# Layer 0 of a four-layer graph network: the general way is chosen before the heads instead of after them

## The chip, the cores and the metric

The kernel runs on one core of a Trainium2 chip. The metric is the device time of one execution in microseconds (us). A core has five engines that run their own instruction queues side by side[...]: TensorE (PE, matrix products; PEld is its weight load), VectorE (DVE), ScalarE (ACT), GpSimd (POOL) and SyncE (SP, which here only starts DMA transfers). Sixteen DMA engines move data between the chip's memory and the core's own buffers. A letter q behind an engine (SPq, ACTq, DVEq) names its sequencer: DMA starts, semaphores, register loads and branches.

## The reference

There are 4096 nodes with 256 features and one 0/1 adjacency matrix of 4096 x 4096, about 0.8% of it ones. Four layers follow each other; each adds its result to its input and normalizes. The change is in layer 0, a graph attention with 8 heads of 32 features:

```
node_feats   = (x @ W.T + b).reshape(4096, 8, 32)
logit_parent = (node_feats * a[None, :, :32]).sum(-1)
logit_child  = (node_feats * a[None, :, 32:]).sum(-1)
attn_logits  = leaky_relu(logit_parent[:, None, :] + logit_child[None, :, :], 0.2)
attn_logits  = where(adj[..., None] != 0, attn_logits, 0.0)
attn_probs   = softmax(attn_logits, axis=1)
out          = einsum('ijh,jhc->ihc', attn_probs, node_feats)
x            = layernorm(x + out)
```

A node that is not a neighbour keeps the logit 0 and so still has weight in the softmax. Layer 1 that follows is `x = layernorm(x + (diagonal(adj) + adj) @ (x @ weight) + bias)`; layers 2 and 3 are not touched by the change.

## The kernel before, in words

Nodes are cut into NB = 32 blocks of P = 128 rows. Layer 0 has two ways to the same result.

**The quick way** uses that exp(leaky_relu(p + c)) is exp(p) exp(c) where p + c is at least 0 and exp(0.2 p) exp(0.2 c) elsewhere, so that the softmax sums become matrix products with masks of zeros and ones. `sums0` (lines 383 to 530) makes the node features, the row factors `fac` (in `factors0`), the number `fits`, the column factors of all heads, written by the ACT queue to the DRAM tensor `gmd`, and then the dense products of the whole adjacency with the small-slope factors: for each pair of row blocks 16 loads of the adjacency, a cast on DVE, a byte copy of the adjacency on ACT stored to `nad` by the POOL queue, and 256 matrix products (line 517). Its result per row block, `zd`, is stored by the ACT queue (line 530). `src`, 132 KB in each partition, is read by these products to the end.

`layer0` (lines 214 to 333) then runs the heads: a loop over the two halves of four heads, in it over four stretches `it` of 1024 rows, in it over the four heads of the half. `na`, the adjacency bytes of a stretch (4 MB in 8 loads), and `gm`, the column factors of the half (6.5 MB in 8 loads, each with all four heads of 4 blocks), are loaded by SP in turns (lines 261 to 264). For a head and a group of 4 column blocks, ACT (groups 0, 1, 3, 4, 6) or DVE (groups 2, 5, 7) compares the row logits with the column logit and writes the mask `sg` (lines 292 and 285), DVE joins it bit by bit with `na` to `gt` (lines 294 and 287), and PE does 32 products of `gt` with `gm` into the accumulator `acc` (line 300),[...] it has two buffers. DVE reduces it, multiplies with `fac`, adds `z` (loaded from `zd` by the POOL queue, line 274) and divides (lines 305 to 316). In the second half the row block is added to `X` and normalized, by POOL during later heads, and for the last stretch by DVE at once (line 331).

**The general way**, `general0` (lines 532 to 690), computes the softmax with its true maxima for every head and row. It is needed only where the exponents would not fit; `fits` says so. It is called in `choose0` (line 335), inside a branch at run time (line 337), which stands between layer 0 and layer 1. There it replaces `X` by its own result. Each engine loads `fits` into a register and takes the branch for itself; where the body is left out, it raises its semaphore by what the body would have added, and SP besides waits for eight DMA counters.

`layer1` (lines 698 to 740) turns each four blocks of `X` (line 108), copies them (line 109), multiplies them by the weight (line 710), splits the product into a rounded and a rest part in `XD` (lines 126 and 127), and then multiplies the adjacency, loaded from `nad` by the ACT queue (line 188) and scaled by DVE and ACT (lines 205 and 203), with `XD` (line 731). The pieces are stored back as `adjs` by SP (lines 160 to 167).

**What sets the order.** The framework's planner orders the instructions of each engine's queue by priority (mostly the order of the program) and by its own estimate of when their inputs are ready; it may move an instruction ahead of older ones that wait. It does not move anything across a run-time branch. Buffers are placed on a stack: a buffer that lies where an older one lay waits for the older one's last user.

Of the kernel before, what the change touches and what calls it, by code (L numbers as in the profile page):

```python
# [9 lines left out]
F32 = mybir.dt.float32  # L10
I32 = mybir.dt.int32
F32R = mybir.dt.float32r
BF16 = mybir.dt.bfloat16
# [10 lines left out]
P = 128  # L24
# [31 lines left out]
class Net:  # L56
# [157 lines left out]
    def layer0(self):  # L214
        nc, tc, NB, D, N = self.nc, self.tc, self.NB, self.D, self.N
        H, C = 8, 32
        C1 = C + 1
        IT = min(1024, N)
        Q = IT // P
        keep = self.ctx.enter_context(tc.tile_pool(name="l0k", bufs=1, space=DRAM))  # L220
        self.fits = keep.tile([1, 1], I32, name="fits")
        with ExitStack() as ctx:
            pool = ctx.enter_context(tc.tile_pool(name="l0", bufs=1))
# [6 lines left out]
            fac = pool.tile([P, 4, NB, H], F32, name="fac")  # L230
            lpd = dram.tile([H, N], F32, name="lpd")

            def row_logits(t, h, it):
                nc.gpsimd.dma_start(t, bass.AP(tensor=lpd.tensor, offset=lpd.offset + h * N + it * IT, ap=[[0, P], [1, IT]]))
                return t
# [5 lines left out]
            zd = dram.tile([NB, P, H, C1], F32, name="zd")  # L241
            yd = dram.tile([NB, P, D // 2], F32, name="yd")
            gmd = dram.tile([2, P, NB, H // 2, 6 * C1], BF16, name="gmd")
            self.sums0(both, nlc, fac, lpd, nad, zd, gmd, lambda: row_logits(first, 0, 0))

            self.open_x()
            self.load1()
            X, xr = self.X, self.rows(self.x)
            gp = ctx.enter_context(tc.tile_pool(name="l0gm", bufs=1))
            work = ctx.enter_context(tc.tile_pool(name="l0w", bufs=2))  # L250
            psum = ctx.enter_context(tc.tile_pool(name="l0ps", bufs=2, space=PSUM))
            K = 4
            gm = gp.tile([P, NB, H // 2, 6 * C1], BF16, name="gm")
# [4 lines left out]
            for half in range(2):  # L258
                for it in range(N // IT):
                    i0 = it * Q  # L260
                    for g in range(NB // K):
                        nc.sync.dma_start(na[:, g * K:(g + 1) * K], nad[it, :, g * K:(g + 1) * K, :])
                        if it == 0:
                            nc.sync.dma_start(gm[:, g * K:(g + 1) * K], gmd[half, :, g * K:(g + 1) * K])
                    if half:
                        nc.sync.dma_start(X[:, i0:i0 + Q, :], xr[:, i0:i0 + Q, :])
                        y0 = work.tile([P, Q, D // 2], F32, name="y0", bufs=1)
# [1 line left out]
                    y = work.tile([P, Q, H // 2, C], F32, name="y")  # L269
                    for hh in range(H // 2):  # L270
                        h = half * (H // 2) + hh
# [48 lines left out]
                    y = y.rearrange("p q h c -> p q (h c)")  # L320
# [5 lines left out]
                    for q in range(0, Q, 2):  # L326
                        xs = X[:, i0 + q:i0 + q + 2, :]
# [4 lines left out]
                        else:  # L332
                            later.append(xs)

    def choose0(self):

        with self.tc.If(self.nc.values_load(self.fits, min_val=0, max_val=1) == 0):
            self.general0()

    def factors0(self, wp, ps, both, nlc, fac):  # L340

# [187 lines left out]
                    nc.vector.tensor_add(zt[:, 0], zt[:, 0], zt[:, 1])  # L529
                    nc.scalar.dma_start(zd[b + q], zt[:, 0])  # L530

    def general0(self):

        nc, tc, NB, D, X = self.nc, self.tc, self.NB, self.D, self.X
        H, C = 8, 32
        C1 = C + 1
        IT = 512
        Q = IT // P
        G = min(8, NB)
        with ExitStack() as ctx:  # L540
            pool = ctx.enter_context(tc.tile_pool(name="l0", bufs=1))
            work = ctx.enter_context(tc.tile_pool(name="l0w", bufs=2))
            nfa = pool.tile([P, NB, H, C1], F32, name="nfa")
            lp = pool.tile([P, NB, H], F32, name="lp")
            lc = pool.tile([P, NB, H], F32, name="lc")
            lc02 = pool.tile([P, NB, H], F32, name="lc02")

            xr = self.rows(self.x)
            for g in range(NB // 4):
                nc.sync.dma_start(X[:, 4 * g:4 * g + 4, :], xr[:, 4 * g:4 * g + 4, :])  # L550

            with ExitStack() as pre:
                wp = pre.enter_context(tc.tile_pool(name="l0pre", bufs=1))
                ps = pre.enter_context(tc.tile_pool(name="l0ps", bufs=2, space=PSUM))
                w0 = self.load_w(wp, self.w0t, "w0")
                b0 = self.load_row(wp, self.b0, "b0")
                a_bc = wp.tile([P, 2, H, C], F32, name="a_bc")
                for s in range(2):
                    nc.scalar.dma_start(
                        a_bc[:, s],  # L560
                        bass.AP(tensor=self.a0.tensor, offset=self.a0.offset + s * C,
                                ap=[[0, P], [2 * C, H], [1, C]]))
                nc.vector.memset(nfa[:, :, :, C:C1].rearrange("p b h c -> p b (h c)"), 1.0)
                for g in range(NB // 4):
                    xT = self.transposed(ps, wp, X[:, 4 * g:4 * g + 4, :], "xT")
                    for q in range(4):
                        b = 4 * g + q
                        pn = ps.tile([P, 512], F32, name="ps_nf")
                        for c in range(2):
                            nc.tensor.matmul(pn[:, :D], xT[:, c, q * P:(q + 1) * P], w0[:, c, :],  # L570
                                             start=(c == 0), stop=(c == 1))
                        nf = nfa[:, b, :, 0:C]
                        nc.vector.tensor_add(nf, pn[:, :D].rearrange("p (h c) -> p h c", h=H),
                                             b0.rearrange("p (h c) -> p h c", h=H))
                        for s, dst in ((0, lp), (1, lc)):
                            prod = wp.tile([P, H, C], F32, name="prod", bufs=2)
                            nc.vector.tensor_mul(prod, nf, a_bc[:, s])
                            nc.vector.tensor_reduce(dst[:, b, :], prod, AX.X, ALU.add)
                nc.vector.tensor_scalar_mul(lc02.rearrange("p b h -> p (b h)"),
                                            lc.rearrange("p b h -> p (b h)"), 0.2)  # L580
# [8 lines left out]
            with tc.For_i(0, NB, Q) as i0:  # L589
# [20 lines left out]
                hz = work.tile([P, Q], F32, name="hz")  # L610
                nc.vector.tensor_scalar(hz, zs[:, :, 0, C], 0.0, -BIG, op0=ALU.is_equal, op1=ALU.mult)

                y = work.tile([P, Q, D], F32, name="y", bufs=1)

                def largest(h):

# [31 lines left out]
                def attend(h, bc, e0):  # L648

                    po = ps_o.tile([C1, IT], F32, name="po")  # L650
                    for g in range(NB // 2):
                        e1 = ep.tile([P, 2, IT], F32, name="e1", bufs=3)
                        e2 = ep.tile([P, 2, IT], F32, name="e2", bufs=2)
                        for k in range(2):
                            jc = 2 * g + k
                            nc.scalar.activation(e2[:, k, :], bc[:, 1, :], AF.Identity, bias=lc02[:, jc, h:h + 1])
                            nc.vector.scalar_tensor_tensor(e1[:, k, :], bc[:, 0, :], lc[:, jc, h:h + 1], e2[:, k, :],
                                                           op0=ALU.add, op1=ALU.max)
                        jc = 2 * g
                        pen = pens[jc // G][:, jc % G:jc % G + 2, :]  # L660

                        nc.vector.tensor_tensor(e1, e1, pen, ALU.min)
                        nc.scalar.activation(e1, e1, AF.Exp)
                        for k in range(2):
                            jc = 2 * g + k
                            nc.tensor.matmul(po, nfa[:, jc, h, :], e1[:, k, :],
                                             start=(jc == 0), stop=(jc == NB - 1))
                    oT = work.tile([C1, IT], F32, name="oT")
                    nc.scalar.copy(oT, po)
                    pt = ps_t.tile([P, 512], F32, name="pt")  # L670
                    for q in range(Q):
                        nc.tensor.transpose(pt[:, q * C1:(q + 1) * C1], oT[:, q * P:(q + 1) * P],
                                            self.ident[:C1, :C1])
                    o = work.tile([P, Q, C1], F32, name="o")
                    nc.vector.tensor_mul(o, zs[:, :, h, :], e0.unsqueeze(2).to_broadcast([P, Q, C1]))
                    nc.vector.tensor_add(o, o, pt[:, :Q * C1].rearrange("p (q c) -> p q c", q=Q))
                    r = work.tile([P, Q], F32, name="r")
                    nc.vector.reciprocal(r, o[:, :, C])
                    nc.vector.tensor_mul(y[:, :, h * C:(h + 1) * C], o[:, :, :C],
                                         r.unsqueeze(2).to_broadcast([P, Q, C]))  # L680

                ahead = largest(0)
                for h in range(H):
                    now, ahead = ahead, (largest(h + 1) if h + 1 < H else None)
                    attend(h, *now)

                xs = X[:, bass.ds(i0, Q), :]
                nc.vector.tensor_add(y, y, xs)
                self.layernorm(work, y, y)
                nc.vector.tensor_copy(xs, y)  # L690


    def load1(self):
# [1154 lines left out]
@with_exitstack  # L1848
def tile_adj_resnorm(ctx: ExitStack, tc: tile.TileContext, args, out: bass.AP):
    net = Net(ctx, tc, args, out)  # L1850
    net.constants()
    net.adj_space()
    net.out_space()
    net.layer0()
    net.choose0()
    net.open_split()
    net.layer1()
    net.layer2()
    net.layer3()
# [41 lines left out]
```

## Time and profile before

| | |
|---|---|
| median of 3 runs | 4065.89 us (4064.93 to 4076.77) |
| the profiled execution | 4074.96 us, its span 4072.8 us |
| busy in the span | PE 96%, PEld 83%, DVE 74%, ACT 68%, POOL 26% |
| dense sums | to 598.0 us (last product of line 517) |
| heads | 613.8 to 1331.2 us (first and last product of line 300) |
| layer 1 | from 1350.1 us (first transpose of line 108) |
| bytes moved | 555.89 MB, mean 136 GB/s |

The profile is one execution. Its times are counted from the start of the span, which lies 2.2 us under the execution's own time; the execution itself lies 9 us above the median of the three runs. A row of the waits reads "who waited, on which line, for whom: us in total, how often, the longest". "issue" stands for time in which the profile shows no awaited engine. A row of the stretches gives from and to, the length, and for each engine its busy time and instructions, then the clock granted to TensorE, the mean busy share of the DMA engines and their GB/s.

### The profile page before, as it was taken

What the parts mean: (1) busy time and instruction counts of PE and PEld (TensorE: products, weight loads), DVE (VectorE), ACT (ScalarE), POOL (GpSimd) and SP (SyncE); (2) the same over time, 40 slices, a digit from 0 to 9 for tenths busy, and PEclk for the clock granted to TensorE, in tenths of its full rate; (3) what the DMA queues carried; (4) which work ended last, traced back from release to release, by engine and by line L of the source; (5) the groups of instructions that cost most, each with busy time, mean ns of one, the idle gap of its engine ahead of it and who ended that gap; (6) DMA issues with size and microseconds to landing.
All of it is one profiled execution on the core that took longest, in us unless ns stands there. A gap on an engine that the chain in (4) does not pass through costs nothing. (4 is left out here: it accounts for less than half of the span.)

```text
span 4072.8 us, 68706 instructions
## 1 busy us (share of the span) xinstructions
PE 3910.6 (96%) x25081; PEld 3381.8 (83%) x25081; DVE 2994.7 (74%) x6647; ACT 2755.4 (68%) x5127; POOL 1073.3 (26%) x1318
## 2 busy tenths in 40 slices
PE   7999989999999799799999999988999999999899
PEld 6999989999999688458888888864888888888677
DVE  7642328999999344548787877847899999999364
ACT  5543329999998222348888888834888888888132
POOL 0111110110333022301111111113455555555211
PEclk9999999999999899899999999999999999999999
DMA  4765555324221497333333333363333333335541
GB/s 122 226 212 177 179 176 189 96 80 148 73 86 48 186 374 306 117 110 92 100 96 95 101 95 103 106 221 96 108 105 117 103 108 115 103 111 190 181 160 47
DMA packets 291193, 555.89 MB, mean 136 GB/s; under 512 B 38966, under 2 KB 115382, under 8 KB 286742
## 3 DMA queue, kind: packets, MB, share of 16 engines
q1 hardware_dynamic: 208672, 394.61, 30.2%
q0 software_dynamic: 27664, 84.44, 6.2%
q10 hardware_dynamic: 54502, 72.27, 5.2%
q8 instruction: 203, 3.33, 0.3%
q14 instruction: 152, 1.25, 0.1%
HBM read 385.25 MB, written 165.94 MB: 135 GB/s over the span
## 5 line engine op out<-in xcount | busy, mean ns | idle before, releaser
L1301 PE MATMUL ps_a<-X,aT 128*128 128x256 f32 x4096 | 972.5, 380 | 1.3 <-ACT h L1442 1.1
L1301 PEld LDWEIGHTS ps_a<-X,aT 128*128 128x128 f32 x4096 | 775.6, 190 | 128.0 <-issue 3.5
L300 PE MATMUL acc<-gm,gt 128*128 128x198 bf16 x8192 | 704.1, 248 | 29.0 <-issue 15.8
L300 PEld LDWEIGHTS <-gt 128*128 128x128 fp8e4 x8192 | 700.4, 97 | 32.6 <-issue 16.0
L292 ACT ACTIVATE sg<-lpb,nlc 128x1024 fp8e4<-128x1024 f32 x640 | 671.3, 1135 | 60.9 <-DVE gt L294 35.0
L179 PE MATMUL ps_r<-XD,adj_piece 128*128 128x512 f32 x1952 | 548.9, 416 | 5.2 <-DMA adj_piece<-adjs 5.2
L517 PE MATMUL pz<-src,ar 128*128 128x264 f32 x4096 | 510.1, 287 | 10.4 <-DVE ar L507 8.2
L517 PEld LDWEIGHTS pz<-src,ar 128*128 128x128 f32 x4096 | 507.2, 190 | 13.2 <-DVE ar L507 12.5
L1028 ACT ACTIVATE ja<-e,nc 128x2048 uint8<-128x2048 f32 x240 | 481.0, 2004 | 2.0
L1294 ACT COPY aT<-ps_tp 128x512 f32<-128x512 f32 x512 | 295.8, 578 | 229.6 <-PE ps_tp L1292 227.5
L179 PEld LDWEIGHTS ps_r<-XD,adj_piece 128*128 128x128 f32 x1952 | 346.3, 190 | 79.3 <-issue 13.4
L510 ACT ACTIVATE nb<-a 128x512 uint8<-128x512 f32 x256 | 156.9, 630 | 292.7 <-DMA a<-in_adjt_dram 288.7
L1093 DVE MAX8 cand<-v 128x8 f32<-128x256 f32 x1024 | 347.2, 412 | 4.4
L1143 DVE SCALAR_TENSOR_TENSOR e<-e,edge 128x512 f32<-128x512 f32 x512 | 347.2, 750 | 2.2
L1292 PE MATMUL ps_tp<-ident,e 128*128 128x128 f32 x2048 | 308.4, 273 | 0.1
L1089 DVE SCALAR_TENSOR_TENSOR v<-e,hi 128x2048 f32<-128x2048 f32 x128 | 300.3, 2346 | 2.4
L1292 PEld LDWEIGHTS ps_tp<-ident,e 128*128 128x128 f32 x2048 | 257.2, 142 | 51.9 <-issue 0.9
L935 PE MATMUL ps_logit<-kT,q 128*128 128x512 f32 x1024 | 277.0, 412 | 15.0 <-DVE kT L893 7.6
L285 DVE TENSOR_SCALAR sg<-lpb,nlc 128x1024 fp8e4<-128x1024 f32 x384 | 283.2, 774 | 2.0
L937 ACT ACTIVATE e<-ps_logit 128x1024 f32<-128x1024 f32 x256 | 259.8, 1025 | 30.5 <-PE ps_logit L935 28.8
L507 DVE CAST ar<-a 128x1024 fp32r<-128x1024 f32 x128 | 88.6, 692 | 230.1 <-PE pz L517 230.0
L731 PE MATMUL ps_adj<-XD,adj_piece 128*128 128x512 f32 x1024 | 236.1, 391 | 0.0
(382 smaller groups left out, 5492.0 us busy)
## 6 DMA issues: line engine op xcount, KB each, us to landing
adj_piece<-adjs SPq DMA_DIRECT2D x552, 256.0 KB
a<-in_adjt_dram SPq DMA_DIRECT2D x256, 256.0 KB
adjs<-adj_piece SPq DMA_DIRECT2D x96, 512.0 KB
na<-nad SPq DMA_DIRECT2D x64, 512.0 KB
nad<-nb POOLq DMA_DIRECT2D x128, 128.0 KB, 3.3
lpb<-lpd POOLq DMA_DIRECT2D x32, 512.0 KB, 4.2
na<-nad ACTq DMA_DIRECT2D x16, 1024.0 KB
gmd<-gb ACTq DMA_DIRECT2D x64, 198.0 KB
```

The costliest lines, as they stand in the source:

```text
L179: nc.tensor.matmul(ps, a[:, k, :], rhs(jc).rearrange("p s d -> p (s d)"), start=(jc == 0), stop=(jc == self.NB - 1))
L285: nc.vector.tensor_scalar(sg[:, k, :], lpb, nlc[:, jc, h:h + 1], 2.0 ** -5, op0=ALU.is_ge, op1=ALU.mult, saturate=False)
L292: nc.scalar.activation(sg[:, k, :], lpb, AF.Sign, scale=-1.0, bias=nlc[:, jc, h:h + 1], saturate=False)
L300: nc.tensor.matmul(acc[:, q, :6 * C1], gt[:, k, q * P:(q + 1) * P], gm[:, jc, hh, :], start=(jc == 0 and q % 2 == 0), stop=(jc == NB - 1 a ...
L517: nc.tensor.matmul(pz[q][:, t, :W], ar[:, q, k, :], src[:, jc, t, s], start=(jc == 0 and s == 0), stop=(jc == NB - 1 and s == 1))
L1028: nc.scalar.activation(ja, e[:, s * HALF:(s + 1) * HALF], f, bias=nc1, accum_out=fs[:, i + s:i + s + 1])
L1089: nc.vector.scalar_tensor_tensor(v, ec, hi, ec, op0=ALU.is_lt, op1=ALU.mult, accum_out=sb[:, s:s + 1])
L1093: nc.vector.max(cand[:, 8 * j:8 * j + 8], v[:, k * 256:(k + 1) * 256])
L1143: nc.vector.scalar_tensor_tensor(ec, ec, edge[:, j:j + 1], ec, op0=ALU.is_ge, op1=ALU.mult)
L1292: nc.tensor.transpose(pt[:, k * P:(k + 1) * P], e[:, jc * P:(jc + 1) * P], self.ident)
L1294: nc.scalar.copy(aT, pt)
L1301: nc.tensor.matmul(pa[:, :D], aT[:, k * P:(k + 1) * P], X[:, jc, :], start=(jc == 0), stop=(jc == NB - 1))
```

## The change

The branch moves from the end of layer 0 to between `sums0` and the heads. The general way no longer writes `X`: it loads its own copies of `x`, writes its attention result, with a one in the 33rd place of each head, to `zd`, clears `gmd` and the two rows of `fac` that scale the head products, and leaves the addition and the norm to the heads. With the products scaled by nothing, the heads divide `z` by one. On the data of this task `fits` is 1 and the body is left out, before and after.

The second part is the order of the loads of `gm`: in each half the factors of its first head are loaded first, in turns with `na`, a group of 4 blocks at a time (for each partition four runs of 396 bytes in place of one of 6336), and then those of the other three heads, 8 blocks at a time.

```diff
             self.sums0(both, nlc, fac, lpd, nad, zd, gmd, lambda: row_logits(first, 0, 0))
+            self.choose0(fac, zd, gmd)
 
             self.open_x()
             self.load1()
...
                     for g in range(NB // K):
                         nc.sync.dma_start(na[:, g * K:(g + 1) * K], nad[it, :, g * K:(g + 1) * K, :])
                         if it == 0:
-                            nc.sync.dma_start(gm[:, g * K:(g + 1) * K], gmd[half, :, g * K:(g + 1) * K])
+                            nc.sync.dma_start(gm[:, g * K:(g + 1) * K, 0], gmd[half, :, g * K:(g + 1) * K, 0])
+                    for hh in range(1, H // 2 if it == 0 else 0):
+                        for g in range(0, NB // K, 2):
+                            nc.sync.dma_start(gm[:, g * K:(g + 2) * K, hh], gmd[half, :, g * K:(g + 2) * K, hh])
...
-    def choose0(self):
+    def choose0(self, fac, zd, gmd):
 
         with self.tc.If(self.nc.values_load(self.fits, min_val=0, max_val=1) == 0):
-            self.general0()
+            self.general0(fac, zd, gmd)
...
-    def general0(self):
+    def general0(self, fac, zd, gmd):
...
-            for g in range(NB // 4):
-                nc.sync.dma_start(X[:, 4 * g:4 * g + 4, :], xr[:, 4 * g:4 * g + 4, :])
-
...
                 for g in range(NB // 4):
-                    xT = self.transposed(ps, wp, X[:, 4 * g:4 * g + 4, :], "xT")
+                    xs = wp.tile([P, 4, D], F32, name="xs", bufs=2)
+                    nc.sync.dma_start(xs, xr[:, 4 * g:4 * g + 4, :])
+                    xT = self.transposed(ps, wp, xs, "xT")
...
-                y = work.tile([P, Q, D], F32, name="y", bufs=1)
+                y = work.tile([P, Q, H, C1], F32, name="y", bufs=1)
+                nc.vector.memset(y[:, :, :, C:], 1.0)
...
-                xs = X[:, bass.ds(i0, Q), :]
-                nc.vector.tensor_add(y, y, xs)
-                self.layernorm(work, y, y)
-                nc.vector.tensor_copy(xs, y)
+                nc.sync.dma_start(zd[bass.ds(i0, Q)].rearrange("b p h c -> p b h c"), y)
+
+            none = pool.tile([P, 4, gmd.shape[-2] * gmd.shape[-1]], BF16, name="none")
+            nc.vector.memset(none, 0.0)
+            for half in range(2):
+                for g in range(NB // 4):
+                    nc.sync.dma_start(gmd[half, :, 4 * g:4 * g + 4].rearrange("p b h c -> p b (h c)"), none)
+            nc.vector.memset(fac[:, 0:2], 0.0)
...
     net.layer0()
-    net.choose0()
     net.open_split()
     net.layer1()
```

More of the change, by code (lines that the diff above doesn't have):

```diff
@@ L530, in sums0 @@
                     nc.scalar.dma_start(zd[b + q], zt[:, 0])
-    def general0(self):
-        nc, tc, NB, D, X = self.nc, self.tc, self.NB, self.D, self.X
+    def general0(self, fac, zd, gmd):
+        nc, tc, NB, D = self.nc, self.tc, self.NB, self.D
         H, C = 8, 32
@@ L540, in general0 @@
         with ExitStack() as ctx:
-            pool = ctx.enter_context(tc.tile_pool(name="l0", bufs=1))
-            work = ctx.enter_context(tc.tile_pool(name="l0w", bufs=2))
+            pool = ctx.enter_context(tc.tile_pool(name="l0n", bufs=1))
+            work = ctx.enter_context(tc.tile_pool(name="l0nw", bufs=2))
             nfa = pool.tile([P, NB, H, C1], F32, name="nfa")
@@ L678, in attend @@
                     nc.vector.reciprocal(r, o[:, :, C])
-                    nc.vector.tensor_mul(y[:, :, h * C:(h + 1) * C], o[:, :, :C],
+                    nc.vector.tensor_mul(y[:, :, h, :C], o[:, :, :C],
                                          r.unsqueeze(2).to_broadcast([P, Q, C]))
```

## The prediction

> **What bounds the kernel now.** The page first: TensorE (PE) is busy for 96% of the span, so time is won only where PE stands still. Its chain of waits holds no waiting worth a per cent. I therefore went by stretches around the two seams of layer 0, then to the waits in each, then to the lines of the branch.
>
> The first seam (dense sums to heads). Columns of the stretches: PE, PE's weight load, VectorE (DVE), ScalarE (ACT) and GpSimd (POOL) busy, granted clock, DMA share, GB/s.
>
> ```profile
> 595.00:600.00 5.00, 2.99 (x25) 2.78 (x23) 3.66 (x11) 1.10 (x1) 0.65 (x1) 1.00 0.18 37
> 600.00:605.00 5.00, 0.00 (x0) 0.00 (x0) 0.74 (x1) 2.23 (x3) 2.29 (x4) 0.55 0.95 349
> 605.00:610.00 5.00, 0.00 (x0) 0.00 (x0) 0.00 (x0) 0.00 (x0) 0.00 (x0) 0.50 1.04 360
> 610.00:615.00 5.00, 1.23 (x8) 1.16 (x9) 2.55 (x4) 3.73 (x4) 0.00 (x0) 0.50 1.01 379
> ...
> 630.00:640.00 10.00, 9.89 (x115) 9.72 (x116) 5.10 (x6) 9.91 (x10) 0.00 (x0) 1.00 1.06 370
> ```
>
> PE has nothing to do from 598.0 to 613.8 while the DMA engines are full, and stay full until 643. The waits between 598 and 665 say what stood in line:
>
> ```profile
> PE acc L300 <- issue: 15.8, 1, 15.8
> ...
> ACT sg L292 <- issue: 9.0, 2, 8.8
> ...
> DVE gt L287 <- DMA na<-nad: 1.2, 1, 1.2
> ```
> and SP's own queue between 560 and 720:
> ```profile
> SPq L262 <- DMA zd<-zt: 7.4, 1, 7.4
> SPq L262 <- DMA w<-in_w_dram: 7.3, 1, 7.3
> ```
>
> ACT makes three masks at 598.9 to 602.5 and stops: its next instruction is the load of w1 (line 115), which starts at 610.29, in the same instant as SP's load that waited for a zd store issued at 599.95. That store needed 10 us behind 3.9 MB of na and gm. The fourth mask, hence the first gt, comes at 612.4 to 613.7. Head 0 ends with the reduction at 642.34; its 256 matmuls at 83.2 ns need 21.3 us. The seam costs 642.3 - 598.0 - 21.3 = 23 us of PE.
>
> The second seam (heads to layer 1), waits between 1325 and 1400, and then the lines of the branch (min/median/max ns, first and last start):
>
> ```profile
> PE ps_tp L108 <- DVEq L337: 19.0, 1, 19.0
> ...
> L337 ACTq COMPARE_BRANCH  x1: 50/50/50, 1315.5 to 1315.5; - x1
> L337 ACTq EVENT_SEMAPHORE  x1: 17/17/17, 1319.5 to 1319.5; - x1
> ...
> L337 PEldq COMPARE_BRANCH  x1: 3447/3447/3447, 1330.2 to 1330.2; - x1
> ...
> L337 DVEq TENSOR_LOAD <-fits x1: 722/722/722, 1346.0 to 1346.0; - x1
> ...
> L337 DVEq COMPARE_BRANCH  x1: 72/72/72, 1346.8 to 1346.8; - x1
> L337 DVEq EVENT_SEMAPHORE  x1: 21/21/21, 1349.8 to 1349.8; - x1
> ```
>
> PE's last head matmul ends at 1331.15, its next instruction starts at 1350.08. Between them DVE runs the last head's closing arithmetic and the norm of the last eight row blocks (to 1346.76), then needs 3.0 us for the branch. PE, ACT and POOL had passed; all wait for DVE, because the branch's body may write X. No engine stops the others at the branch; each loads fits itself, jumps, and counts itself through.
>
> [...] 2.9 us on DVE, 3.9 on ACT, 3.4 on PE. [...] the hardware queues' single packets take 13 ns at 128 B, 18 at 256, 27 at 512, 46 at 1024, 67 at 1584, 159 at 4096 and 241 at 6336 (medians of the packet records), a straight line. [...] the trace shows 0.50 in both pauses.
>
> **The change, part by part.**
>
> *First seam, wait added.* Everything behind the branch that uses memory of the general way, or reads zd and gmd, waits until the engines are through it. PE: 1331.15 to 1333.8 before, so 598.0 + 2.7 = 600.7. DVE: last zt 599.92 + 3.0 = 602.9. ACT: its last instruction is the zd store issued at 599.95 (ends 600.28), then load 0.65, branch[...]: 605.0. SP: it must see all outstanding hardware DMAs land (it waits on eight counters there), the zd store among them[...]. POOL is idle from 588. Last is ACT: na's first load starts at 605.0 instead of 598.87, 6.1 us later. Queued behind: all na and gm loads on SP, z and lpb loads on POOL, the w1 and bias loads and the masks on ACT.
>
> *First seam, wait removed.* The zd stores have landed before any load starts, so the 7.4 us hold of SP and the 7.8 us hold of ACT go. ACT: w1 and bias issues (0.41 + 0.49) then masks without a pause, 4.28 us per group of four (1.07 each). Groups 0, 1, 3, 4, 6 are ACT's: ready at 606 + 4.28 x 1..5 = 627.4, plus 1.23 for gt. PE takes groups in order at 2.66 us; group 6 from 628.6, group 7 ends at 634.
>
> *First seam, loads.* Head 0 needs na (4 MB: 1024 packets x 159 ns / 16 engines = 10.2 us) and its own quarter of gm in runs of 396 B. Between 256 and 512 B the records give 23 ns: 4096 x 23 / 16 = 5.9 us. With lpb and z (about 3 us) that is 19 us: all there at 605 + 19 + 2 = 626, before group 7 needs it at 631. Before it was 10.2 + 15.4 us and later. Bounds of a run: 18 ns, and 46 (as dear as 1 KB; 11.8 us, data at 632, still no loss over 1). The other heads' gm is 12 DMAs per half behind it, 17.7 us, needed from 634 on; hidden under head 0 and 1. SP issues 12 more DMAs in each half (28 for 16); at 0.32 to 0.55 us each (the 256-run loads of line 957 take 0.55) that is under 7 us of a queue which then idles until 681. ACT and DVE no longer have a lead over PE when PE starts, and both are over 96% busy in the first half, so I take 2 us off for hiccups. Head 0 ends at 634 to 636 against 642.3: gain 6. Bounds: 0 (first load at 611) and 9.
>
> *Half change.* Before: PE 100% busy from 900 to 1000. The new loads of the first head need 16 us instead of 26 and are released group by group over a head of 21 us. Cost 0; uncovered it would be a few us, once.
>
> *Second seam.* No branch, and X is not written by the general way: groups 0 to 5 of layer 1 (row blocks 0 to 23, last normed by POOL at 1298) can be turned and multiplied while DVE finishes. Their buffers: the accumulator's banks of head 30 are free since 1313; XD lies over fac and gm, read last at 1333.7. So PE idles 2 to 3 us rather than 19. Layer 1's eight groups took 1350.1 to 1373.6, 2.9 us each; six fill 17.6 us, the last two wait for the norm, which gets slower by the 24 split subtractions of 0.42 us on DVE (10 us, into a stretch of 15.6 where DVE is busy 11.7). End of the groups: 2.6 + 8 x 2.9 = 26 us after PE's last head matmul, against 42.5: 16; I take 2 off, because the layer's first pieces wait for na loads (DMA share 0.9 to 1.0 from 1350 to 1390, DVE waited 10.4 us for na) which gain less than PE. Gain 14. Bounds: 3.0 (only the branch goes) and 20 (PE never cold).
>
> *The general way itself* (its loads of x, its store to zd, cleared gmd and fac) doesn't run: fits is 1, as the trace shows no instruction of it.
>
> *Sum.* 6 + 14 = 20. The profiled execution took 4074.96 us (span 4072.8, 2.2 around it): 4055. It lies 9 above the median of the runs, 4065.89, so the forecast there is 4046.
>
> **The rivals.**
>
> (a) *The second seam stays shut*: layer 1 still waits for the whole norm, by the order the planner writes or by memory. For it: one queue per engine, ACT's na loads may stand before its copies. Against: after the branch, products and support are already mixed line by line. Only the branch is saved: 6 + 3 = 9, 4057.
>
> (b) *The first seam doesn't pay*: the loads start 6 us later and head 0 ends 6 later than now, at 648. For it: DMA share 1.0 up to 643. Against: the bytes wanted first fall from 10.5 to 5.6 MB. 14 - 6 = 8, 4058.
>
> (c) *More*: PE stays warm at the second seam and ACT passes the branch as fast as DVE: 9 + 20 = 29, 4037.
>
> (d) *Slower*: small runs become the bound. Place: head 0 of each half. At y ns per run its data come at 605 + 13 + 0.256y + 2 and are wanted at 631; at the half change the slack is some 25 us. The loss 0.512y - 36 eats the 20 at y = 109 ns and makes it 12 us slower at y = 133, some six times the 23 that the records give. For it: no packet of this size on these queues. Against: the straight line from 128 to 6336 B. With y = 135: 4079.
>
> **How the numbers follow.** Forecast 0.68 (4038 to 4053), (c) 0.08, (a) 0.12, (b) 0.05, (d) 0.07. About 0.3% or 12 us is what a measurement of this kernel can tell from no change; the three runs of before themselves spread by 12. Faster: 0.68 + 0.08 = 0.76; same: (a) + (b) = 0.17; slower: (d) 0.07. The range 4033 to 4060 leaves out (d), a third of (c), and the worse part of (a) and (b): under 0.15.
>
> **What would show it.** The branch's lines near 584 to 605; first na load at 605, first gt at 610 to 612, no 7 us waits for zd or w; head 0's reduction at 634 to 637; lines 108 and 710 start within 3 us of the last head matmul while DVE still norms; no PE wait for a branch there. Wrong if ACT is held again after the branch, if gm packets take far over 23 ns, if the transposes of layer 1 stand behind the last norm, or if the planner puts layer 1's copies among the last heads' masks and PE falls under 95% there.

## The result: 0.28% faster, little more than half of what was forecast

| | before | after |
|---|---|---|
| median of 17 runs each, side by side | 4070.23 us (4062.77 to 4076.77) | 4056.93 us (4049.9 to 4069.3) |
| ratio, 95% interval | | 0.9972 (0.9965 to 0.9979), 11.4 us less |
| the profiled execution | 4074.96 us | 4049.9 us |

The forecast was 20 us less. The time measured, 4057, is in the stated range, and it is the time that rival (a) gives, "6 + 3 = 9, 4057". To the microsecond that is luck: the rival counts from the 4065.89 us of three runs, and beside 17 runs the kernel before took 4070.23. In differences the forecast was 20, rival (a) 9, and 11.4 was measured.

The two profiled executions lie 24.6 us apart in their spans, twice the real difference. So the profiles were cut at marks that both kernels have, and the stages compared one by one:

| stage (us) | before | after | difference | forecast |
|---|---|---|---|---|
| last dense product to head 0's reduction | 44.34 | 39.67 | -4.7 | -6 |
| head 0's reduction to the last head product | 688.77 | 687.95 | -0.8 | 0 |
| last head product to layer 1's last adjacency product | 302.35 | 294.12 | -8.2 | -14 |
| the rest (layers 2 and 3) | 2439.4 | 2430.1 | -9.3 | 0 |

The first three rows make 13.7 us, inside the interval of the ratio (8.5 to 14.2 us). The fourth is not the change's: nothing is changed there, and before, after and the seven kernels below, whose layers 2 and 3 are the same, spread from 2426.5 to 2439.4 in it. The dense sums also happened to end 1.7 us sooner (596.3 against 598.0).

**The profile after.** From the page: the busy line, and the group of the head products.

```profile
PE 3903.3 (96%) x25081; PEld 3379.7 (83%) x25081; DVE 2995.7 (74%) x6647; ACT 2757.0 (68%) x5127; POOL 1072.1 (26%) x1318
...
L304 PE MATMUL acc<-gm,gt 128*128 128x198 bf16 x8192 | 704.3, 249 | 23.3 <-DVE gt L298 15.9
```

The shares are those of before: a change of 0.3% can't be read from them. (Lines have moved: the products of the heads are line 304 now, na's load is 263, gm's are 265 and 268, the branch is 341, layer 1's first products are 718 and its adjacency products 739.)

The first seam of after, in stretches with the columns of the prediction:

```profile
595.00:600.00 5.00, 1.32 (x11) 1.10 (x9) 2.98 (x9) 0.00 (x0) 0.00 (x0) 0.99 0.19 61
600.00:605.00 5.00, 0.00 (x0) 0.00 (x0) 0.75 (x1) 1.27 (x2) 2.72 (x4) 0.50 0.35 99
605.00:610.00 5.00, 0.69 (x5) 0.63 (x6) 1.97 (x3) 5.00 (x6) 0.48 (x1) 0.50 1.02 268
610.00:615.00 5.00, 4.24 (x29) 3.78 (x28) 2.47 (x3) 5.00 (x6) 0.00 (x0) 0.64 1.05 347
615.00:620.00 5.00, 4.12 (x49) 4.11 (x49) 2.68 (x3) 5.00 (x6) 0.00 (x0) 1.00 1.09 352
620.00:630.00 10.00, 10.00 (x121) 10.00 (x119) 9.87 (x13) 9.91 (x10) 0.00 (x0) 1.00 1.16 322
```

The waits of after between 598 and 665, and under them those of SP's queue between 560 and 720:

```profile
PE acc L304 <- DVE gt L298: 13.0, 1, 13.0
...
DVE gt L291 <- DMA na<-nad: 3.8, 1, 3.8
...
PE acc L304 <- DMA gm<-gmd: 1.6, 1, 1.6
DVE gt L298 <- DMA na<-nad: 1.0, 1, 1.0
```
```profile
SPq L341 <- SPq L341: 18.9, 5, 13.2
...
SPq L263 <- DMA w<-in_w_dram: 1.8, 1, 1.8
```

PE starts 13.0 us after the dense sums, before it was 15.8. The two holds of SP (7.4 us for zd, 7.3 for w) have shrunk to one of 1.8, and ACT is full from 605 on. But PE is not: DVE waits 4.8 us in all for na and PE 1.6 us for gm. With the DMA engines full (share 1.02 to 1.16 from 605), the loads are now a part of what head 0 waits for.

The branch in after (min/median/max ns, first and last start):

```profile
L341 SPq EVENT_SEMAPHORE  x8: 17/17/17, 582.8 to 601.5; - x8
...
L341 PEldq COMPARE_BRANCH  x1: 3555/3555/3555, 594.8 to 594.8; - x1
...
L341 ACTq COMPARE_BRANCH  x1: 58/58/58, 599.4 to 599.4; - x1
L341 DVEq EVENT_SEMAPHORE  x1: 21/21/21, 601.7 to 601.7; - x1
L341 ACTq EVENT_SEMAPHORE  x1: 17/17/17, 602.1 to 602.1; - x1
```

ACT is last, at 602.1, and na's first load starts at 602.19: 5.9 us after the sums. SP's last wait at the branch ends at 601.5.

The second seam of after, waits between 1300 and 1390, and then PE and ACT in order of time (start, duration, what it is, in brackets the idle time before it and its releaser):

```profile
ACT xT L109 <- POOL ln_rstd L89: 26.1, 1, 26.1
...
PE ps_sup L718 <- ACT xT L109: 13.5, 1, 13.5
```
```profile
1325.89 1.06 PE L108 MATMUL ps_tp<-ident,X 128*128 128x128 f32 x8 [1.95 <-issue]
1340.48 3.72 PE L718 MATMUL ps_sup<-w,xT 128*128 128x256 f32 x8 [13.53 <-ACT xT L109]
```
```profile
1339.84 0.59 ACT L109 COPY xT<-ps_tp 128x512 f32<-128x512 f32 x1 [26.06 <-POOL ln_rstd L89]
1339.88 0.33 ACTq L188 DMA_DIRECT2D na<-nad  x1
```

The branch's 19.0 us wait is gone, and PE turns the first group of X 1.95 us after the last head product (1323.94). Then it stands for 13.5 us. The group is turned at 1327; ACT has been idle since 1313.8; still it copies the group to xT only at 1339.84, when the norm of the last row blocks has done with its small tiles (`ln_rstd` is one). The data of that norm are not in this group.

### The profile page after: what moved, and what is told of

It is laid out like the page before. It is cut to its first block, busy times and chain, and to the rows that moved or that the text cites. A ratio compares the mean times of both kernels' runs of the same rounds, so it can differ in the third digit from the quotient of the medians.

```text
span 4048.2 us, 68758 instructions
## 1 busy us (share of the span) xinstructions
PE 3903.3 (96%) x25081; PEld 3379.7 (83%) x25081; DVE 2995.7 (74%) x6647; ACT 2757.0 (68%) x5127; POOL 1072.1 (26%) x1318
```

## The experiments

Each was run in five rounds (5 to 22 executions) beside the kernel before, in two batches. Ratios are to the kernel before of the same batch: own_xT, branch_only, order_only and no_branch to 4072.05 us, own_tail, held and held_tail to 4070.63. The last three columns, in us, come from one profile each.

| kernel | median us | ratio (95%) | sums to head 0's reduction | last head product to first product of layer 1 | to its last adjacency product |
|---|---|---|---|---|---|
| before, after | 4070.23, 4056.93 | 0.9972 (0.9965 to 0.9979) | 44.34, 39.67 | 20.79, 16.54 | 302.35, 294.12 |
| own_xT | 4058.61 | 0.9968 (0.9957 to 0.9979) | 39.20 | 3.25 | 290.74 |
| branch_only | 4068.24 | 0.9992 (0.9986 to 0.9999) | 47.44 | 16.54 | 295.43 |
| order_only | 4064.86 | 0.9985 (0.9978 to 0.9992) | 38.22 | 21.03 | 303.92 |
| no_branch | 4057.05 | 0.9964 (0.9953 to 0.9975) | 38.84 | 16.54 | 297.03 |
| own_tail | 4054.26 | 0.9955 (0.9941 to 0.9969) | 39.79 | 3.25 | 286.95 |
| held | 4065.49 | 0.9989 (0.9983 to 0.9996) | 37.14 | 16.54 | 293.75 |
| held_tail | 4056.40 | 0.9967 (0.9956 to 0.9978) | 36.99 | 3.25 | 287.73 |

How well one profile repeats is seen where kernels have the same code. The first seam took 39.2 to 39.8 us in after, own_xT and own_tail; the last column reads 293.8 to 297.0 in after, branch_only, no_branch and held. Kernels that lie 11 to 15 us under the kernel before can't be told apart by these intervals.

### own_xT: the buffer for which ACT waits, in a pool of its own

```diff
+            turned = ctx.enter_context(tc.tile_pool(name="l1x", bufs=2))
             work = ctx.enter_context(tc.tile_pool(name="l1w", bufs=2))
...
-                xT = self.transposed(psum, work, X[:, 4 * g:4 * g + 4, :], "xT")
+                xT = self.transposed(psum, turned, X[:, 4 * g:4 * g + 4, :], "xT")
```

> The changed kernel, with the turned copy xT of layer 1 in a pool of its own, laid ahead of the pool of layer 1's other buffers, so that its memory lies over gm and na only and no longer shares a pool with memory that the last norm still uses. Theory (memory keeps the second seam shut): the first products of line 710's kind start within 4 us of the last head product, not 16.5 us after it; 6 to 10 us faster than the changed kernel, so 17 to 22 us under the kernel before. Rival (DVE sets the end: the split subtractions delay the norm, and the last two groups wait for it): the products start early but layer 1 ends no more than 2 us sooner than in the changed kernel; 11 to 14 us under the kernel before.

PE and ACT of own_xT in order of time; its last head product ends at 1326.80:

```profile
1330.05 3.51 PE L719 MATMUL ps_sup<-w,xT 128*128 128x256 f32 x8 [0.24 <-ACT xT L109]
...
1338.46 1.13 PE L719 MATMUL ps_sup<-w,xT 128*128 128x256 f32 x4 [2.64 <-DVE XD L127]
1341.08 3.78 PE L719 MATMUL ps_sup<-w,xT 128*128 128x256 f32 x8 [1.48 <-DVE XD L127]
```
```profile
1329.41 1.07 ACT L109 COPY xT<-ps_tp 128x512 f32<-128x512 f32 x2 [12.76 <-PE ps_tp L108]
```

The copy now waits for its input, and layer 1's products start 3.25 us after the last head product instead of 16.54. In the programs built from after and own_xT the two xT buffers lie at the same addresses, over `na` (bytes 82976 to 91168 of a partition; `na` has 79392 to 112160), and `na` was read to its end before. So the 13.3 us came from no data and from no place in memory: they came from the pool. The pool `l1w`, which holds xT in after, reaches to byte 190724 and so also covers the heads' working tiles, the norm's small ones (167712 to 168008) among them. That the pool decides is shown; that the framework frees all of a pool's memory as one is inferred. The sentence ahead of the prediction, that a buffer waits for the last user of the older one at its place, is too narrow by this.

Yet layer 1 ends only 3.4 us sooner (290.74 against 294.12), and the ratio can't be told from that of after. On the time, 13 us under the kernel before, the rival was right and not the theory, though the layer ends more than the rival's 2 us sooner. PE's idle time between the last head product and the layer's last adjacency product says why (from the records of its products; the clock's part is half of the time at work in the stretches that the trace's clock records give as 0.50: in own_xT eight products of line 719 took 3.78 us at 0.50, from 1341.08, and 1.89 us at 1.00, from 1348.32):

| | before | after | own_xT | own_tail |
|---|---|---|---|---|
| PE idle, us | 22.7 | 15.8 | 8.9 | 7.9 |
| PE at work, us | 279.6 | 278.3 | 281.9 | 279.1 |
| of it lost to the clock, us | 2.4 | 1.8 | 4.5 | 1.6 |

Opening the pool took 6.9 us of idle time, not 13.3: the products that PE could start soon wait for DVE's split (line 127), which stands behind the norm. And PE's time at work became 3.5 us longer, most of it because its clock fell a second time. Stretches of 2 us in own_xT:

```profile
1330.00:1332.00 2.00, 1.95 (x5) 1.58 (x6) 1.90 (x6) 0.48 (x1) 0.00 (x0) 0.50 0.00 0
...
1342.00:1344.00 2.00, 2.00 (x6) 1.55 (x6) 1.14 (x3) 0.81 (x3) 0.21 (x1) 0.50 0.00 0
1344.00:1346.00 2.00, 2.00 (x7) 1.53 (x6) 0.45 (x2) 0.91 (x3) 0.00 (x0) 0.50 0.00 0
```

The clock's part is 2.7 of the 3.5 us. Without it the time at work is 276.5 to 277.5 us in all nine profiles, so the rest is of the size by which these profiles differ.

### own_tail: own_xT, with DVE relieved of a part of the last norm

```diff
-                        engine.tensor_add(xs[:, :, :D // 2], xs[:, :, :D // 2], y0[:, q:q + 2])
+                        nc.gpsimd.tensor_add(xs[:, :, :D // 2], xs[:, :, :D // 2], y0[:, q:q + 2])
...
-                            self.layernorm(work, xs, xs)
+                            mv, rstd = self.moments(work, xs)
+                            shift = work.tile([P, 2], F32, name="ln_shift")
+                            nc.gpsimd.tensor_scalar_mul(shift, mv[:, :, 0], -1.0)
+                            nc.gpsimd.tensor_tensor(shift, shift, rstd, ALU.mult)
+                            for k in range(2):
+                                nc.scalar.activation(xs[:, k, :], xs[:, k, :], AF.Identity,
+                                                     bias=shift[:, k:k + 1], scale=rstd[:, k:k + 1])
```

> The changed kernel with xT in its own pool (as in own_xT) and with part of the last norm taken off DVE: the additions of the first half's result go to POOL, scaling and shifting to ACT, which is idle there; DVE keeps the statistics and the additions of the second half. About 4.4 us of DVE work leave the 15 us after the last head product. Theory (with the memory open, DVE is next: its queue holds the norm ahead of layer 1's split subtractions): from last head product to last adjacency product of layer 1 3 to 5 us less than in own_xT's 290.7, so 286 to 288; 16 to 19 us under the kernel before. Rival (layer 1 is set by the na loads, which wait for the last user of the heads' buffers, or by PE's cold clock): within 1.5 us of own_xT.

Stretches of 2 us in own_tail, whose last head product ends at 1332.17:

```profile
1336.00:1338.00 2.00, 2.00 (x6) 1.61 (x5) 1.97 (x7) 0.00 (x0) 0.00 (x0) 0.50 0.00 0
...
1344.00:1346.00 2.00, 0.00 (x0) 0.00 (x0) 0.00 (x0) 1.54 (x5) 0.87 (x3) 1.00 0.00 0
1346.00:1348.00 2.00, 1.16 (x5) 1.06 (x6) 0.85 (x2) 0.70 (x3) 0.00 (x0) 1.00 0.47 98
```

The layer ends 3.8 us sooner than in own_xT, after 286.95 us, as the theory said. But only 1.0 of the 3.8 us is idle time, and in held_tail, which has the same seam, the idle time is own_xT's 8.9. The other 2.8 us are time at work, and the clock accounts for them: the 4.5 us of own_xT are 1.6 here (1.7 in held_tail), since the clock falls once and not twice. So the edit paid by the clock; that DVE's work was the next limit of PE's idle time isn't shown. The trace shows a new wait in its place (waits between 1325 and 1390, then ACT in order of time):

```profile
DVE XD L127 <- ACT XD L126: 25.9, 23, 4.5
...
PE ps_sup L725 <- DVE XD L127: 4.3, 4, 3.4
```
```profile
1344.98 1.09 ACT L340 ACTIVATE X<-X,ln_shift,ln_rstd 128x256 f32<-128x256 f32 x2 [0.46 <-POOL ln_shift L338]
1345.98 0.35 ACT L126 CAST XD<-ps_sup 128x256 fp32r<-128x256 f32 x1
```

The norm's scaling (L340) now stands in ACT's queue ahead of layer 1's rounding (L126), for which DVE's split waits up to 4.5 us, and PE up to 3.4 us for the split, until 1346.84.

This is the fastest of the kernels measured, 0.9955; its interval overlaps that of after. That its two edits together pay in time is shown by another pair, held and held_tail: 0.9989 and 0.9967, with intervals that don't overlap.

### branch_only and order_only: each part of the change alone

```diff
 (branch_only: after, with the old order of the loads)
-                            nc.sync.dma_start(gm[:, g * K:(g + 1) * K, 0], gmd[half, :, g * K:(g + 1) * K, 0])
-                    for hh in range(1, H // 2 if it == 0 else 0):
-                        for g in range(0, NB // K, 2):
-                            nc.sync.dma_start(gm[:, g * K:(g + 2) * K, hh], gmd[half, :, g * K:(g + 2) * K, hh])
+                            nc.sync.dma_start(gm[:, g * K:(g + 1) * K], gmd[half, :, g * K:(g + 1) * K])
```

order_only is the kernel before with the opposite edit.

> The changed kernel with the old order of the gm loads (eight loads with all four heads in each). Theory (the order of the loads is what pays at the first seam, the branch costs there): head 0's reduction 8 to 11 us later than in the changed kernel, since na and all of gm are 10.5 MB instead of 5.6 MB; about 3 to 6 us under the kernel before. Rival (the seam gains because ACT is no longer held by w1's load, not by the order of the loads): head 0 within 3 us of the changed kernel; 9 to 12 us under the kernel before.

> The kernel before with the new order of the gm loads, the branch where it was. Theory (the order pays by itself): head 0's reduction 6 to 10 us earlier than before, the second seam unchanged at 20.8 us from last head product to first product of layer 1; 5 to 9 us under the kernel before. Rival (ACT's hold on w1's load sets head 0, whatever the order): head 0 within 3 us of before, same time.

Waits of branch_only between 598 and 668, then of order_only:

```profile
PE acc L301 <- DMA gm<-gmd: 18.1, 3, 14.6
...
DVE gt L288 <- DMA na<-nad: 6.7, 2, 3.9
...
DVE gt L295 <- DMA na<-nad: 5.9, 3, 3.4
```
```profile
PE acc L303 <- issue: 12.3, 1, 12.3
...
ACT sg L295 <- issue: 5.6, 2, 5.3
```

The order of the loads alone gives 6.1 us at the first seam (44.34 to 38.22) and 0.15% in time, about 6 us. The branch alone costs 3.1 us there (44.34 to 47.44): with the old order its delay of the loads falls on loads that PE waits for at once (18.1 us for gm). With the new order it costs 1.5 (38.22 to 39.67). At the second seam its removal starts the products 4.25 us sooner and ends the layer 6.9 us sooner (302.35 to 295.43). So the gain at the first seam is the order's, and that at the second is the branch's. Both theories came close: branch_only ends head 0 7.8 us later than after (8 to 11 expected) and is 3.3 us under the kernel before (3 to 6); order_only is in all its ranges. The prediction credited a part of the first to the branch, which clears the zd stores and so ends ACT's hold. The hold is still there in order_only (5.3 us), and head 0 ends sooner than in after all the same.

### no_branch: after without the general way

```diff
-            self.choose0(fac, zd, gmd)
```

> The changed kernel without the branch and the general way (left out altogether). It prices the branch at its new place. Theory (the branch costs the first loads some 5 us there): first na load about 1 us after the last dense product instead of 6, head 0 3 to 5 us earlier, 3 to 5 us under the changed kernel, 14 to 17 under the kernel before. Rival (the zd stores hold the loads again, as in the kernel before, when no branch makes SP wait for them): no gain over the changed kernel, 10 to 13 us under the kernel before.

0.9964 against 0.9972 for after, with intervals that overlap; at the first seam it is 0.8 us shorter, not the theory's 3 to 5 (the time, 15 us under the kernel before, is in the theory's range). na's first load does start 0.9 us after the dense sums, but one line of its ACT queue shows the rival's hold, which the branch had cleared, w1's load, which starts 7.1 us after the last zd store (601.81):

```profile
608.94 0.41 ACTq L115 DMA_DIRECT2D w<-in_w_dram  x1
```

So what the branch costs where it now stands is about 1 us by the first seam; the times, 3 us apart, can't tell it from none. The first product of layer 1 comes after 16.54 us here too: the wait that is left at the second seam has nothing to do with the branch.

### held and held_tail: the other heads' factors loaded during the heads

In held, the loads of head hh + 1's factors stand at head hh in the program, and row logits and z of the first stretch are loaded by SP, behind the loads of head 0. held_tail is own_tail with the same edit. The loads of w1 and the bias stay on ACT's queue, beside those of head 0.

```diff
-                    for hh in range(1, H // 2 if it == 0 else 0):
-                        for g in range(0, NB // K, 2):
-                            nc.sync.dma_start(gm[:, g * K:(g + 2) * K, hh], gmd[half, :, g * K:(g + 2) * K, hh])
...
-                        lpb = row_logits(work.tile([P, IT], F32, name="lpb"), h, it) if h or it else first
+                        queue = nc.gpsimd if half or it else nc.sync
+                        lpb = row_logits(work.tile([P, IT], F32, name="lpb"), h, it, queue) if h or it else first
                         z = work.tile([P, Q, C1], F32, name="z")
-                        nc.gpsimd.dma_start(z, zd[i0:i0 + Q, :, h].rearrange("b p c -> p b c"))
+                        for g in range(0, NB // K if it == 0 and hh + 1 < H // 2 else 0, 2):
+                            nc.sync.dma_start(gm[:, g * K:(g + 2) * K, hh + 1], gmd[half, :, g * K:(g + 2) * K, hh + 1])
+                        queue.dma_start(z, zd[i0:i0 + Q, :, h].rearrange("b p c -> p b c"))
```

> The changed kernel with the loads of the first stretch of the first half in one queue: the row logits of heads 1 to 3, the z of heads 0 to 3 and the gm of head h + 1 are traced in head h and issued by SP behind the na and gm loads of head 0, so that no other transfer shares the DMA engines with head 0's first loads. Theory (head 0 loses some 5 us because 1.6 MB of row logits, z, w1 and bias cross with its loads: DVE waited 3.8 us for na, PE 1.6 us for gm): from last dense product to head 0's reduction 36 to 37.5 us instead of 39.7, 2 to 3 us under the changed kernel. Rival (ACT's pace of 4.3 us per group sets head 0): within 1 us of 39.7; and if the row logits of head 1 come late, a longer head 1.

> own_tail and held together. If both theories hold, their gains add: first seam 36 to 37.5 us, second seam and layer 1 286 to 288 us, 18 to 22 us under the kernel before. If the rivals hold, as own_xT: 11 to 14 us under it.

A wait of held between 598 and 680, and its SP queue in order of time:

```profile
ACT sg L296 <- DMA lpb<-lpd: 9.0, 1, 9.0
```
```profile
620.62 8.10 SPq L277 DMA_DIRECT2D gm<-gmd  x4
628.77 1.53 SPq L278 DMA_DIRECT2D z<-zd  x1
630.34 1.44 SPq L234 DMA_DIRECT2D lpb<-lpd  x1
```

Head 0 ends after 37.14 us, 2.5 sooner than in after. So the 2.5 us were lost to what crossed the loads of na and gm there and is moved here: two loads each of row logits and z by the POOL queue (1.3 MB). w1 and the bias still cross. But head 1 then takes 31.70 us instead of 23.11: its row logits are queued behind four loads that hold SP for 8.1 us, and ACT waits 9.0 for them. held gives back more than three times what it won, and instead of 2 to 3 us under after it lies 7 above (0.9989). held_tail has the same long head 1 (32.05 us), and its 13 us under the kernel before are those of the rival, not the theory's 18 to 22: the gains didn't add.

## Why the prediction was wrong, point by point

**First seam: right, 1.3 us short.** Forecast 6, measured 4.7. The branch itself was cheaper than worked out: ACT through after 5.8 us instead of 7.0, the first load at +5.9 instead of +7.0, with 2.7 us between ACT's jump and its count (599.45 to 602.15) where 3.9 was taken from before. A run of 396 B took 24 ns (median of the packet records) for the 23 taken, so rival (d) falls by a factor of five. The other heads' factors were indeed hidden: heads 1 and 2 took 23.11 and 21.38 us, before 22.14 and 23.68. What was left out is the order in which loads land: the sum has "about 3 us" for lpb and z and asks only when all are there. DVE and PE waited 6.4 us for single loads, and held shows that 2.5 us of what crossed them reached the end of head 0. The step "the 7.4 us hold of SP and the 7.8 us hold of ACT go" was right as a fact and worth little: order_only keeps ACT's hold and ends head 0 1.5 us sooner after the sums than after does.

**Half change: right.** From the 16th to the 17th reduction 24.65 us before, 24.15 after.

**Second seam: the step that failed.** It reads: "Their buffers: the accumulator's banks of head 30 are free since 1313; XD lies over fac and gm, read last at 1333.7. So PE idles 2 to 3 us rather than 19." It asked of the accumulator and of XD when they come free, each by its own last reader, and did not ask it of xT at all. xT was the one that waited, for the last user of everything under its pool: PE's first product came after 16.54 us instead of 2 to 3. Given a pool of its own, xT let the product start after 3.25 us (own_xT). Rival (a) had named it, "by the order the planner writes or by memory", and it was memory. It got 0.12 because the order seemed to argue against it, and the order was no evidence on memory.

**Second seam, a reading that was wrong.** "Layer 1's eight groups took 1350.1 to 1373.6, 2.9 us each": the groups ran to 1402.2. A group has 8 turns and 16 products, and the lines' groups give 9.8 and 33.6 us for all eight, so 5.4 us of PE each; and adjacency products are mixed in from 1358.9. The sum 2.6 + 8 x 2.9 = 26 measured a stage that doesn't exist in this form. What can be won at this seam is PE's idle time in the whole layer, 22.7 us. Of that the change took 6.9, and 1.3 us came from PE's time at work. The 6.9 are 3.5 in the first 20 us (19.0 to 15.5), close to the lower bound "3.0 (only the branch goes)", and 3.4 later in the layer (3.7 to 0.3). The later part isn't steady: branch_only, no_branch and held, with the same seam, have 1.2, 2.8 and 0.2 there, and their layers are 6.9, 5.3 and 8.6 us shorter than before. So the layer gains some 5 to 9 us by the removal of the branch, and 8.2 is near the upper end.

**What lay behind it.** Would the forecast have held with xT free? own_xT: 13.8 us of idle time gone, close to the 14; but the layer shorter by 11.6 only, since the clock took 4.5 us of PE's time at work, broken by pauses, and not 2.4. The prediction had the reason for waiting ("the 24 split subtractions of 0.42 us on DVE") and no price for the clock. Of the last 7.9 us of idle time in own_tail, 3.4 lie behind the norm's scaling on ACT. What keeps the rest isn't settled: no run took away the loads of na, which begin 13.9 us after the last head product there (1346.1).

## What to carry to other kernels

Before a pause is counted as filled, go through every buffer that the first instruction of the next stage writes, and ask for the last user of the whole pool under it, not of the buffer that lay at its address. Before a gain is put down for a moved wait, sum PE's idle time over the whole stage, and price the clock beside it: a stage that is filled with work broken by pauses can run at a lower clock and give a part back (4.5 us of own_xT's layer 1, 2.4 of before's). An engine that takes work over from another has a queue too, and what stands behind the new work waits (in own_tail DVE's split, up to 4.5 us). When loads are put in the order of need, those of other queues that cross them count too (2.5 us of head 0 in after), and a small load behind large ones on a queue costs what they cost (in held ACT waited 9.0 us for row logits behind loads that held SP for 8.1).

## What was not expected of the hardware

The branch had no one price. From the end of an engine's jump to its count behind it passed, in before and after, 2.84 and 2.96 us on DVE, 3.94 and 2.70 on ACT; on POOL it was 0.13 us in before; on PE the jump itself took 3.45 and 3.56. What fills this time isn't shown. The load of the register ahead of it took 0.65 to 0.80 us.

PE's clock followed the pauses late, and not all of them. At the two seams of before it fell to 0.50, 2.5 and 3.2 us after PE's last product (at 600.5 and 1334.4 by the clock records), and was back at 1.00 3.8 and 4.8 us after the next one. At the first seam of after the two delays were 3.6 and 4.2 us; at the second it fell 3.0 us after the last head product, behind the eight products that turn the first group of X, and was back 3.5 us after the first product of layer 1's line 718. In own_xT it was at 0.50 from 1342 to 1346, where PE was busy all the time, after pauses of 2.6 and 1.5 us; in own_tail it stayed at 1.00 through a pause of 3.4 us (1343.5 to 1346.8) and after it. What decides isn't shown: no run moved a pause on purpose.
